# Attention, a 1.58-bit feed-forward and retention joined into one loop over tiles

## The chip, the cores and the metric

The kernel runs on one core of a Trainium2 chip. A core has five engines that work side by side, each through its own instructions in order: TensorE (PE, matrix products and transposes, with weight loads listed apart as PEld), VectorE (DVE), ScalarE (ACT), GpSimd (POOL) and SyncE (SP, which issues transfers). They share the on-chip memory SBUF; products go into PSUM[...]. The metric is the device time of one execution in microseconds (us); lower is better.

## The reference

Four layers, each a gated cross attention and a gated feed-forward, are added onto x, 16 sequences of 128 tokens by 256 features in 32-bit floats. The change touches the second layer and the first half of the third:

```python
x = x + tanh(g_xattn[0]) * L0_xattn(ctx, ctx, layernorm(x), ...)   # long convolution
x = x + tanh(g_ffn[0])   * L0_ffn(layernorm(x), ...)               # mixture of 8 experts, 2 per token
x = x + tanh(g_xattn[1]) * L1_xattn(layernorm(x), ctx, ctx, mask)  # grouped attention, 16 heads on 4
x = x + tanh(g_ffn[1])   * L1_ffn(layernorm(x), w1, w2, w3)        # 1.58-bit feed-forward
x = x + tanh(g_xattn[2]) * L2_xattn(layernorm(x), ctx, ctx, decay) # retention
x = x + tanh(g_ffn[2])   * L2_ffn(layernorm(x), ...)               # mixture of 8 experts, 2 per token
x = x + tanh(g_xattn[3]) * L3_xattn(layernorm(x), ctx, ...)        # attention, 16 heads of 8
x = x + tanh(g_ffn[3])   * L3_ffn(layernorm(x), ...)               # mixture of low-rank experts

# L1_ffn, d = 256, hidden 704
act_quant(x)    = clip(round(x * s), -128, 127) / s,  s = 127 / max(max|x| over a row, 1e-5)
weight_quant(w) = clip(round(w * s), -1, 1) / s,      s = 1 / max(mean|w|, 1e-5)
bitlinear(x, w) = act_quant(x) @ weight_quant(w).T
L1_ffn(x) = bitlinear(silu(bitlinear(x, w1)) * bitlinear(x, w3), w2)

# L2_xattn: a running sum over the 128 tokens of a sequence
r[t] = decay * r[t-1] + ctx[t] * ctx[t]
out[t] = layernorm(x)[t] * r[t]
```

## The kernel before

x stays in SBUF for the whole run as 16 tiles (one a sequence, 128 tokens on the partitions, 256 features). Each half layer is a stage with pools of its own, and the stages follow one another in `passage`: the long convolution (`stage_l0x`), the first mixture (`stage_moe0`), grouped attention (`stage_l1x`), the 1.58-bit feed-forward (`stage_l1f`), retention (`stage_l2x`), the second mixture (`stage_moe2`), the last attention and the last mixture. Most stages write the order of PE, DVE and ACT out by hand (`tc.manual_schedule`): an engine does its instructions in the order in which the functions below are called. POOL's and SP's instructions are placed by the scheduler. A second passage follows only where a flag asks for it.

`stage_l1x` is a loop over steps n. A step does for several tiles a part of the work each: statistics and normalisation of tile n + 4 (`stats`, with the collecting of the first mixture's results, L736, `normal`, L1032), for each pair of tiles the transposes and queries (`turn_x`, `queries`, L1050), the scores and their Exp of tile n (`weigh`, L1092 and L1095, in two halves of two PSUM banks each), the mix with the values of tile n - 1 (`mix`, L1101), its normalisation (`normalise`, L1109 to L1114), the turn and output product of tile n - 2 (`turn_o`, L1120; `output`, L1129 and L1131). Scores use two PSUM buffers of two banks (pool `pss`), everything else four of one bank (pool `pst`). Beside it, one piece a step, `quant_weights` loads the feed-forward's three weight matrices (L1189), sums their absolute values (L1198) and rounds them to -1, 0 and 1 in three DVE instructions each (L1208, L1212, L1220).

`stage_l1f` is a loop of its own with three PSUM buffers of two banks and two of one: statistics on DVE, the reciprocal root on POOL (L1259), normalisation on POOL (L1262), largest absolute value (L1266) and scale, rounding on ACT by adding a large constant (L1281), transposes (L1290) and a copy that takes the constant away (L1294), two products up (L1304), Silu on ACT (L1317), gate on DVE (L1320), largest value and scale (L1322 to L1325), rounding of the hidden rows on ACT (L1330), six transposes (L1337), copy (L1341), product down (L1347) and output (L1351).

`stage_l2x` has no order by hand: it squares the transposed context on ACT (L1388), makes a decay row (POOL L1384, DVE L1386), scans along time on DVE (L1390), and for each pair of tiles transposes the result (L1399), multiplies (L1405) and adds (L1406); its layer norm is the shared helper (L155 to L163). The second mixture's weights (`moe2_weights`, L134 and L141, six transfers from POOL's queue) are held back by `after_all` until the attention's output of tile 5.

## Time and profile before

| What | us |
|---|---|
| median of 3 runs (lowest, highest) | 1083.84 (1081.39, 1085.41) |
| time of the profiled execution | 1083.83 |
| its span | 1082.1 |
| attention: first scores to end of last output | 349.3 to 477.1 |
| feed-forward: its own loop | 477.1 to 566.5 |
| retention | 566.5 to 599.2 |
| second mixture's first DVE instruction | 599.2 |
| all of PE, DVE, ACT, POOL busy, share of the span | 83%, 56%, 40%, 34% |

The profile's page shows each engine's busy share in 40 equal slices, 27 us each. Attention, feed-forward and retention lie in slices 13 to 22:

```profile
PE   3899978999999999966652558899169999998796
DVE  5988867322225465448979859554346555435342
PEclk9999989999999999988995557999569999998899
```

A digit is the busy share in tenths. PE and DVE change places: where PE reads 9, DVE reads 4 to 6, and where DVE reads 7 to 9, PE falls to 6, 5 and 2. The last row is the clock that PE was granted.

### The profile page before, as it was taken

How to read it: one execution, taken by the hardware profiler on the slowest of the kernel's cores; microseconds unless marked ns; L12 is line 12 of the kernel's file. 1: busy time of each engine (PE TensorE's matmuls, PEld its weight loads, DVE VectorE, ACT ScalarE, POOL GpSimd, SP SyncE). 2: the span in 40 equal slices, each digit the busy share in tenths (PEclk: the TensorE clock that was granted, in tenths of full speed). 3: DMA queues.
4: the chain of work that ended last, by engine and by line, in shares of the span. 5: the costliest groups of instructions: out<-in, count | busy, mean ns of one | idle time of the engine just before them, and what ended most of it. 6: DMA issues, size and time to landing. Idle time of an engine off the chain costs nothing. (4 is left out here: it accounts for less than half of the span.)

```text
span 1082.1 us, 14956 instructions
## 1 busy us (share of the span) xinstructions
PE 900.1 (83%) x5212; PEld 595.4 (55%) x5212; DVE 610.3 (56%) x1508; ACT 436.2 (40%) x662; POOL 366.3 (34%) x417
## 2 busy tenths in 40 slices
PE   3899978999999999966652558899169999998796
PEld 1444466777778445424432558788145555555564
DVE  5988867322225465448979859554346555435342
ACT  2111033233322444437760134455257888881111
POOL 5756232643024334035511116650443343201000
PEclk9999989999999999988995557999569999998899
DMA  9100080233223109000000100443489787620000
GB/s 310 34 0 1 0 233 6 78 107 105 65 66 122 40 30 200 1 0 1 1 1 0 59 19 26 151 147 88 124 227 271 216 230 204 169 62 1 20 30 32
DMA packets 71403, 94.13 MB, mean 87 GB/s; under 512 B 9271, under 2 KB 63127, under 8 KB 69015
## 3 DMA queue, kind: packets, MB, share of 16 engines
q1 hardware_dynamic: 56952, 67.21, 20.8%
q0 software_dynamic: 14080, 23.78, 10.3%
q10 hardware_dynamic: 288, 2.10, 0.5%
q8 instruction: 45, 0.74, 0.3%
q14 instruction: 38, 0.31, 0.1%
HBM read 57.06 MB, written 33.55 MB: 84 GB/s over the span
## 5 line engine op out<-in xcount | busy, mean ns | idle before, releaser
L1634 ACT ACTIVATE pt<-s 128x1024 f32<-128x1024 f32 x128 | 127.2, 1024 | 27.5 <-PE s L1627 23.8
L717 POOL DMA_INDIRECT yc<-ys,pos x64 | 62.1, 971 | 129.5 <-DVE x L736 55.2
L297 PE MATMUL y<-kv,toep 128*128 128x512 f32 x192 | 85.7, 597 | 2.3 <-DVE toep L237 2.3
L1643 PE MATMUL av<-pt,v 128*32 128x256 f32 x1024 | 69.4, 389 | 0.1
L289 POOL TENSOR_TENSOR kv<-ctxT 128x1024 f32<-128x1024 f32 x32 | 60.1, 1898 | 27.5 <-PE y L297 27.5
L1627 PE MATMUL s<-qa,ka 64*128 64x256 f32 x512 | 64.9, 334 | 3.4 <-ACT pt L1634 2.7
L1627 PEld LDWEIGHTS s<-qa,ka 64*128 64x128 f32 x512 | 39.0, 190 | 41.5 <-issue 18.3
L297 PEld LDWEIGHTS y<-kv,toep 128*128 128x128 f32 x192 | 35.5, 190 | 44.4 <-issue 41.0
L1654 DVE COPY avs<-av 128x256 f32<-128x256 f32 x64 | 27.1, 423 | 56.4 <-PE av L1643 55.4
L601 POOL DMA_INDIRECT xb<-xs,who x40 | 38.1, 952 | 41.1 <-PE tb L613 32.9
L624 PE MATMUL ub<-L0we,xbT 128*128 x160 | 50.7, 460 | 0.2 <-ACT xbT L615 0.2
L920 PE MATMUL yb<-L2we,hT 88*128 (+1 forms) x224 | 41.2, 312 | 6.4 <-DVE hT L744 4.6
L855 POOL DMA_INDIRECT xb<-xs,who x40 | 38.1, 952 | 24.9 <-PE tb L867 14.9
L1534 POOL TENSOR_TENSOR hl<-f,hl 128x512 fp32r<-128x512 f32 x16 | 20.5, 1280 | 74.3 <-ACT hl L1533 74.3
L302 DVE TENSOR_TENSOR pr<-y,qT 128x1024 f32<-128x1024 f32 x32 | 39.0, 1222 | 11.2 <-PE y L297 9.4
L1095 ACT ACTIVATE pt<-s 128x1024 f32<-128x1024 f32 x32 | 32.8, 1024 | 25.3 <-PE s L1092 25.2
L485 PE MATMUL up<-L0s,xT 128*128 128x352 f32 x128 | 42.5, 477 | 0.0
L920 PEld LDWEIGHTS yb<-L2we,hT 88*128 88x128 f32 x224 | 33.2, 202 | 13.2 <-DVE hT L744 10.1
L305 DVE TENSOR_REDUCE oT<-pr 128x128 f32<-128x1024 f32 x32 | 38.9, 1220 | 1.0
L1643 PEld LDWEIGHTS av<-pt,v 128*32 128x32 f32 x1024 | 26.9, 110 | 20.5 <-issue 0.9
L650 PE MATMUL yb<-L0we,hTb 88*128 x160 | 37.9, 379 | 0.0
L624 PEld LDWEIGHTS ub<-L0we,xbT 128*128 128x128 f32 x160 | 28.8, 190 | 13.2 <-ACT xbT L615 0.5
(383 smaller groups left out, 2031.1 us busy)
## 6 DMA issues: line engine op xcount, KB each, us to landing
scr<-hl SPq DMA_DIRECT2D x64, 256.0 KB, 2.6
ys<-ysb SPq DMA_DIRECT2D x40, 256.0 KB, 2.1
qa<-scr SPq DMA_DIRECT2D x32, 256.0 KB, 4.7
ka<-scr SPq DMA_DIRECT2D x32, 256.0 KB, 5.2
L2we<-in_L_w_dram POOLq DMA_DIRECT2D x6, 792.0 KB, 7.1
L0we<-in_L_w_dram SPq DMA_DIRECT2D x6, 704.0 KB, 7.2
xs<-xn SPq DMA_DIRECT2D x8, 512.0 KB, 4.0
ctxT<-in_ctxT_dram ACTq DMA_DIRECT2D x2, 1024.0 KB, 5.9
```

The costliest lines, as they stand in the source:

```text
L289: nc.gpsimd.tensor_tensor(t, bc(ch, 3, 8), bc(ch, 2, 8), ALU.mult)
L297: nc.tensor.matmul(y[:, ns], lhsT=T[:, h, d : d + P], rhs=kv[mc][:, ns], start=(mc == 0), stop=(mc == lc))
L302: nc.vector.tensor_tensor(pr, y.rearrange("p (b j i) -> p b j i", b=B, j=8), bc(qT[:, lc, :, hs], 2, 8), ALU.mult)
L305: nc.vector.tensor_reduce(oT[:, lc, :, hs], pr, AX.X, ALU.add)
L485: nc.tensor.matmul(t[:, n, 0 : 2 * I], lhsT=xT[:, c, b * P : (b + 1) * P], rhs=s13[:, c, n, :], start=(c == 0), stop=(c == 1),)
L601: nc.gpsimd.indirect_dma_start(out=xbs[s][:, i, :], out_offset=None, in_=xs, in_offset=bass.IndirectOffsetOnAxis(ap=who[:, 2 * s + i : 2 * ...
L624: nc.tensor.matmul(t[:, i, 0 : 2 * I], lhsT=xbT[:, i, c, :], rhs=we[:, bass.ds(regs[s][i] + c * 2 * I, 2 * I)], start=(c == 0), stop=(c == 1),
L717: nc.gpsimd.indirect_dma_start(out=got[b][:, i, :], out_offset=None, in_=ys, in_offset=bass.IndirectOffsetOnAxis(ap=pos[:, i, b : b + 1], ...
L920: nc.tensor.matmul(y[:, i, :], lhsT=hT[:, x, k, i, :], rhs=we[0:HI, bass.ds(at[i] + 4 * I + k * D, D)], start=(n == 0), stop=(n == 3),)
L1627: nc.tensor.matmul(s[:, h, jj, :], lhsT=ka[r, 2 * i + jj, sc * P : (sc + 1) * P], rhs=qa[r, 2 * i + jj, :], start=True, stop=True,)
L1634: nc.scalar.activation(pts[b, i][:, sc], s, AF.Exp)
L1643: nc.tensor.matmul(av[c : c + 32, :], lhsT=va[:, sc, 8 * h + 2 * i + jj, :], rhs=pt[:, sc, h, jj, :], start=(sc == 0), stop=(sc == 1),)
```

## The change

The two loops after the attention go away as stages of their own. `following` gives two functions that the attention's loop calls in each of its steps: `begun(n)`, which quantises the weights in steps 1 to 5, squares the context in steps 1 and 2, makes decay and scan in steps 6 and 7 and issues the second mixture's weights in step 8; and `then(m, place)`, which at four places of a step does the feed-forward and retention of a pair of tiles, by a table `order` of (distance, place). A pair starts every second step and passes through six distances. The loop runs four steps longer. In detail:

- the feed-forward's normalisation goes from POOL to DVE;
- the products up are made in halves of 352 columns (first and third weights side by side in one buffer), so Silu and gate come as four instructions a pair of tiles, twice two halves;
- products up and hidden transposes take the attention's two score buffers; the other products and transposes take its four small ones;
- small scales of two tiles are made in one instruction, and retention multiplies and adds by tile, not by pair;
- three matrices and the decay rows lie in the space of the first mixture's weights, smaller tiles in that of its transposed input; context, its square and the scan share one place;
- the second mixture's weights wait for no chosen instruction, but for the space that the matrices and decay rows held.

```diff
-    def stage_l1x(wq, wo, ka, vbuf, collect, work, pieces):
+    def stage_l1x(wq, wo, ka, vbuf, collect, work, follow):
...
-            for n in range(-4, B + 3 + e):
+            begun, then = follow(pss, pst)
+            for n in range(-4, B + 7 + e):
                 p, odd = divmod(n, 2)
                 fill()
                 when(turn_o, n - e - 2)
+                then(n - e, 0)
...
                 when(stats, n + 4)
                 when(mix, n - e - 1)
+                then(n - e, 1)
...
+                then(n - e, 2)
                 when(output, n - e - 2)
                 when(weigh, n - e, 0)
                 if not odd:
                     when(queries, p + 1, 0, n=B // 2)
                 when(normalise, n - e - 1)
                 when(weigh, n - e, 1)
-                if pieces and not work:
-                    pieces.pop(0)(pst)
...
+                if n >= 0:
+                    begun(n)
+                then(n - e, 3)
...
+            def begun(n):
+                if n == 0:
+                    assert not work
+                    layout()
+                elif n < 4:
+                    total(n - 1)
+                    if n < 3:
+                        squared(n - 1)
+                    else:
+                        size()
+                elif n == 4:
+                    integers(0)
+                    integers(1)
+                elif n == 5:
+                    integers(2)
+                elif n < 8:
+                    decayed(n - 6)
+                    scanned(n - 6)
+                elif n == 8:
+                    l2we.append(moe2_weights())
...
+            def integers(i):
...
+                nc.vector.tensor_scalar(flat[i], flat[i], v["sum"][:, i, 1:2], MAGIC, ALU.mult, ALU.add)
+                nc.vector.tensor_scalar(flat[i], flat[i], MAGIC, 1.0, ALU.subtract, ALU.min)
+                nc.vector.tensor_scalar(w.rearrange("p n w -> p (n w)"), flat[i], -1.0, None, ALU.max)
...
+            def up(q, i):
+                a13 = v[f"a13{q % 2}"]
+                for n in range(2):
+                    t = pss.tile([P, 2, 512], F32, name="fu", tag="s")
+                    for k in range(2):
+                        for c in range(2):
+                            nc.tensor.matmul(
+                                t[:, k, 0:352],
+                                lhsT=v["xT"][:, c, i * P : (i + 1) * P],
+                                rhs=wq[k][:, c, n * 352 : n * 352 + 352],
+                                start=(c == 0),
+                                stop=(c == 1),
+                            )
+                    nc.scalar.activation(v[f"sil{n}"], t[:, 0, 0:352], AF.Silu, scale=a13[:, 0, i : i + 1])
+                    nc.vector.scalar_tensor_tensor(
+                        v[f"hid{i}"][:, n * 352 : n * 352 + 352],
+                        t[:, 1, 0:352],
+                        a13[:, 1, i : i + 1],
+                        v[f"sil{n}"],
+                        ALU.mult,
+                        ALU.mult,
+                    )
...
+            def turn_hidden(q, i):
+                t = pss.tile([P, 8, P], F32, name="fh", tag="s")
+                for n in range(6):
+                    nc.tensor.transpose(t[:, n, :], v[f"hid{i}"][:, n * P : (n + 1) * P], ident)
+                nc.scalar.activation(v[f"hT{i}"], t[:, 0:6, :], AF.Identity, bias=v["magic"][:, 1:2])
...
+            def retain(q):
+                t = pst.tile([P, 2, 2, P], F32, name="fr", tag="a")
+                for i in range(2):
+                    b = 2 * q + i
+                    for c in range(2):
+                        nc.tensor.transpose(t[:, i, c, :], ctxT[:, c, b * P : (b + 1) * P], ident)
+                x = x_of(q)
+                for i, xn in enumerate(rn.pop(q)):
+                    nc.vector.tensor_tensor(xn, xn, t[:, i].rearrange("p c s -> p (c s)"), ALU.mult)
+                    nc.vector.scalar_tensor_tensor(x[:, i, :], xn, tg[:, 2:3], x[:, i, :], ALU.mult, ALU.add)
...
+            order = {
+                (0, 3): [lambda q: stats(q, "f")],
+                (1, 0): [lambda q: normal(q, "f", [v["xn"][:, i, :] for i in range(2)]), largest],
+                (1, 1): [rounded],
+                (1, 3): [turn],
+                (2, 0): [lambda q: up(q, 0)],
+                (2, 1): [lambda q: up(q, 1)],
+                (3, 0): [lambda q: hidden(q, 0), lambda q: hidden(q, 1)],
+                (3, 1): [lambda q: turn_hidden(q, 0)],
+                (3, 2): [lambda q: turn_hidden(q, 1)],
+                (4, 2): [down],
+                (5, 0): [lambda q: stats(q, "r")],
+                (5, 1): [retain_normal],
+                (5, 3): [retain],
+            }
+
+            def then(m, place):
+                for (d, at), fs in order.items():
+                    q, odd = divmod(m - 3 - d, 2)
+                    if at == place and not odd and 0 <= q < B // 2:
+                        for f in fs:
+                            f(q)
```

## The prediction

> **What bounds the kernel now.** I read the page's slices first, then busy time by stretch around the change, then the waits inside those stretches. Columns of the stretches: length, busy time of PE, PE's weight loads, DVE, ACT and POOL (instructions in brackets), granted PE clock, DMA share, GB/s.
>
> ```profile
> 376.00:392.00 16.00, 15.95 (x74) 7.79 (x72) 10.56 (x27) 7.43 (x12) 4.43 (x5) 1.00 0.08 24
> 497.00:547.00 50.00, 35.18 (x243) 24.14 (x241) 46.20 (x138) 36.95 (x50) 25.55 (x48) 0.98 0.00 1
> 477.00:566.50 89.50, 54.34 (x352) 35.66 (x352) 70.73 (x208) 56.04 (x74) 42.50 (x76) 0.91 0.00 1
> 566.50:599.20 32.70, 8.11 (x32) 6.14 (x32) 30.59 (x43) 3.70 (x2) 5.97 (x5) 0.50 0.00 0
> ```
>
> Three limits follow one another. One pair of attention tiles (first row, two steps of the loop) has PE without a gap and DVE at 66%. The feed-forward has DVE at 92% in its steady part and over its 89.5 us PE at 61%. Retention is DVE alone. After the attention's last output (it ends at 477.1) 122 us pass until the second mixture's first DVE instruction at 599.2. The waits, in the attention (first line) and in the feed-forward's steady part (the others), show who is slack; columns: who waited for whom, us in total, times, longest.
>
> ```profile
> DVE xn L1032 <- POOL rs L1023: 16.3, 10, 2.3
> PE y L1347 <- ACT hT L1341: 8.3, 10, 1.1
> PE th L1337 <- ACT hq L1330: 6.1, 10, 1.1
> DVE hid L1320 <- ACT sil L1317: 1.1, 2, 0.7
> ```
>
> In the attention DVE waits 1.6 us each time for POOL's power (POOL issues two gathers first). In the feed-forward PE waits for ACT and DVE, never the reverse for long. A timeline of ACT at the feed-forward's start (start, length, what) gives a price that the new order will pay often:
>
> ```profile
> 487.94 1.09 ACT L1281 ACTIVATE xq<-xn,magic,inv 128x256 f32<-128x256 f32 x2 [1.68 <-DVE inv L1270]
> 489.05 1.28 ACT L1317 ACT_TABLE_LOAD   x1
> 490.34 0.85 ACT L1317 ACTIVATE sil<-ph,a 128x704 f32<-128x704 f32 x1
> ```
>
> Exp and Silu need different tables; before, each stage switches once.
>
> **What the Trainium skill says.** "ScalarE: Activation LUTs", What ACT_TABLE_LOAD costs: a switch is a load of about 1283 ns and a drain of about 1380 ns. The load agrees (1.28 us); the Silu starts 0.01 us after it, so no drain is paid here, and I take 1.28. "TensorE: Matmul & The Clock Gate", Part 1: an idle array drops to half clock and regains it under load. It agrees: 0.50 in retention, 1.00 in the attention. "Perfetto Trace Analysis", Optimization Strategy: a gap that repeats on the engine that should be full can mean too few PSUM buffers. No stretch before shows it, but the change puts the feed-forward into the attention's two score buffers.
>
> **The change, part by part.** The attention's steps 4 to 17 get the other two stages' work, a pair of tiles every two steps; steps 18 to 22 finish it. On PE's first work of a step (its turn of the output, L1120) I read where steps start: 4 at 379.1, 8 at 410.6, 14 at 457.9, 16 at 469.8. A steady attention pair thus takes 15.75 us, the pair of 14 and 15 takes 11.9, the last 7.3.
>
> PE, added per pair of tiles: 4 turns of x, 12 of the hidden and 4 of the retained, at 0.11 us (six take 0.64): 2.2; 16 products up at 0.15 (eight take 1.2): 2.4; 12 down at 0.09 (six take 0.55): 1.1. Together 5.7; a full pair is 15.75 + 5.7 = 21.5.
>
> DVE per pair: the attention's own is 10.56 less two weight sums of 1.61, so 7.3. Added: two statistics at 1.3 (two of 0.42, two of 0.18, one 0.17) 2.6; two normalisations of two tiles at 0.41, 1.65 (the feed-forward's was POOL's, 1.23 each; that relief of POOL is worth nothing by itself); the largest, 0.68 + 3 x 0.17 = 1.2; the gate in halves, 4 x 0.58 (between the same operation's 0.48 at 256 and 0.95 at 704), two maxima at 0.88, three small at 0.16: 4.55; two outputs 0.96; retention 2 x 0.42 + 2 x 0.48 = 1.8. Sum 12.75, with the attention's 20.0. Two of the powers stand right before their use (0.9 and 1.2 us): 22.1. So DVE passes PE and becomes the bound of the mix.
>
> ACT per pair: 7.4 + 6.9 (36.95/50 of 9.3) + 0.3 for halved Silus + two table loads 2.6 = 17.2. Covered by DVE's 22.1, but the load lies between a product up and its gate; the cover is then PE's next product, and uncovered it is 1.28 us a pair.
>
> Steady pair: the feed-forward alone kept DVE 92% busy, so 22.1/0.92 = 24.0, and 0.5 for the table load: 24.5. The single pairs:
> Steps 4, 5: PE 15.75 + 0.4 + 2.4 = 18.6. In step 4 DVE rounds two weight matrices at once, 2 x (1.09 + 1.03 + 0.88) = 6.0, and PE's first product up waits for them, 5.5 after the turn that covers it; the third matrix (2.9) costs 1.5 more. 26.
> Steps 6, 7: DVE 7.3 + 0.8 + 1.2 + 4.55 + 1.0 + 1.3 = 16.1 and two decays and scans, 2 x (1.28 + 4.41) = 11.4: 27.5, taken as 28.
> Steps 8 to 11: 2 x 24.5 = 49.
> Steps 12, 13: no more collecting and normalising for the attention (4 x 0.48, 1.5 and 0.8): DVE 15.8, so PE bounds: 21.5/0.92 = 23.5.
> Steps 14, 15: PE 11.9 + 5.7 = 17.6; with waits 19.5.
> Steps 16, 17: little attention is left; a pair's own chain bounds, from its power to the turned input 7 us, then the products up through two buffers, their maximum and scale 7, and two of waits: 16.
> Sum 162. Start at 379.1 + 2 (two squares of 1.9 us on ACT in steps 1 and 2, between an Exp and the copies that PE needs; at least 0, at most 4): 381. Step 17 ends at 543.
>
> The tail is the last pair alone: 7 to its turned input; 7 for the products up (each half goes 0.6 on PE, 0.48 ACT, 0.58 DVE with three hand-offs, 2.2 us through two buffers, so 1.1 a half) with maximum and scale; 7 for two roundings (0.97), turns, copies (0.90), 12 products and two outputs; 5 for statistics, power, normalisation and retention; 1 for a PE at half clock. 27. The end is 570 against 599.2: 29 us gone. The profiled execution took 1083.83 (span 1082.1), as good as the median 1083.84: 1083.83 - 29 = 1055.
>
> Bounds of the unknown: DVE without any gap. Its work from 379 on is now 52.7 (376 to 477) + 70.7 + 30.6 = 154, and 10 more (16 normalisations 6.6, cut instructions 3.4): 164. Less the tail's 20, 144 after 381, and 27: 552, a gain of 47. That is the best. The worst is priced under the rivals.
>
> Edits at nothing: the weights of the second mixture are issued after step 7's scan, about 435, instead of 410 to 423. They took until 440 (DMA was full from 400 to 440) and the first use is at 629.9, so 130 us cover them. On POOL's queue six issues of 1.04 us and the wait for the scan stand before later gathers; three gather buffers cover a step. If not, 5 us. The weights to be rounded go into the first mixture's space, free since its last product at 309. Padding and decay memsets, 1.9 us of POOL, lie under the start. What follows from 599 on isn't touched and moves as a whole; its first PE work runs at half clock as before, since the tail leaves PE mostly idle.
>
> **Rivals.** First: DVE is packed densely, because the two stages lack each other's stalls. For it: DVE's waits for the attention's products (25.6 us) now have other work in them; against: the clumps in steps 4 to 7 and a strict order. End 554, time 1038. Second: a pair takes 28, since POOL's powers and ACT's tables add to DVE instead of hiding. Five pairs by 3.5 and 5 in the tail: 592, time 1077. Third, slower: the two PSUM buffers that scores, products up and hidden turns share. Each of six hand-offs a pair makes PE wait for ACT and DVE: Silu 0.48, gate 0.58, hand-offs 0.6, about 1.7 us. That is 10 on a mean PE load of 19.8 over seven pairs, 7 x 30 = 210: 381 + 210 + 27 = 618, 19 slower, 1103. It decides from 1.25 us a hand-off (step 17 at 572, so 27.3 a pair and 7.5 of waits). For it: with three such buffers the feed-forward alone already had PE waiting 0.8 us for the hidden copy. Against: attention work stands between most uses, and scores never made PE wait with two. That the stages don't interleave at all is excluded, since the order is written out per step.
>
> **How the numbers follow.** Forecast 1055 (1042 to 1068) 0.56; dense DVE 0.17; 28 a pair 0.15; buffers 0.12. The range leaves out the last and the far half of the dense one: 1034 to 1082. A measurement here tells 0.5%, 5.4 us. Faster: 0.56 + 0.17 + half of 0.15 and a little = 0.82; same 0.05; slower 0.13.
>
> **What would show it.** DVE near 90% and PE near 88% busy from step 8 to 13, with 24 to 25 us a pair; 13 or 14 table loads in the loop; PE idle about 5 us before the first product up; scans followed by a late DVE; the second mixture's first DVE instruction near 570. PE waiting on the gate or the hidden copy over 1 us in most steps would show the third rival; PE at 99% in the mix would show that I overrate DVE's part, and a pair of 28 or more with neither full, that waits in series were underrated.

## The result, and the profile after

The changed kernel takes 1069.1 us (median of 4 runs, 1067.99 to 1071.18), the kernel before on the same chip 1084.05: a ratio of 0.987, with a 95% interval of 0.984 to 0.989. So 15 us are gone where the forecast had 29. In the profiled execution (1067.99 us, span 1066.2) the second mixture's first DVE instruction stands at 583.59 instead of 599.19, which is 15.6 us earlier; the spans differ by 15.9, so what follows it only moved. The loss against the forecast of 570 must therefore lie in the loop and its tail.

The first view of the changed kernel is busy time by stretch, one row for each pair of steps from step 4 on and the last row for the tail. The columns are those of before: stretch, length, PE, PE's weight loads, DVE, ACT, POOL, granted PE clock, DMA share, GB/s.

```profile
383.40:411.20 27.80, 22.86 (x94) 11.05 (x94) 20.54 (x54) 11.54 (x19) 7.21 (x11) 0.73 0.07 19
411.20:439.20 28.00, 22.04 (x116) 12.44 (x117) 23.81 (x52) 17.10 (x25) 7.23 (x11) 0.94 0.07 20
439.20:472.00 32.80, 25.00 (x120) 14.20 (x120) 25.05 (x60) 16.61 (x25) 12.62 (x16) 0.84 1.27 157
472.00:496.20 24.20, 21.36 (x121) 12.55 (x122) 19.05 (x58) 16.57 (x25) 3.86 (x8) 1.00 0.00 1
496.20:519.80 23.60, 21.30 (x121) 12.46 (x121) 15.46 (x46) 16.86 (x25) 2.49 (x6) 1.00 0.00 1
519.80:540.90 21.10, 18.83 (x101) 10.28 (x102) 14.48 (x44) 15.44 (x22) 2.48 (x6) 0.92 0.00 1
540.90:559.20 18.30, 12.64 (x83) 8.48 (x84) 14.47 (x44) 12.33 (x18) 2.48 (x6) 1.00 0.01 2
559.20:583.60 24.40, 12.36 (x72) 8.11 (x69) 18.77 (x53) 9.06 (x13) 3.88 (x8) 0.85 0.00 0
```

The reader sees at once which row stands out. Steps 10 and 11 (fourth row) are the steady pair and take 24.2 us. Steps 8 and 9 (third row) do the same work on the tiles, with the second decay and scan (5.7 us of DVE) besides, and take 32.8. PE is busy 88% of the steady pair and DVE 79%, so no engine is full. Where the clock is under 1.00, the same matmuls also cost PE more time: 25.00 us in the third row, 21.36 in the fourth.

The waits of the same stretches (who waited for whom, us in total, times, longest) name what PE lacked:

```profile
PE s L1083 <- ACT follow L1375: 10.2, 5, 5.8
PE fu L1339 <- DVE follow L1347: 8.3, 7, 2.0
PE fu L1339 <- DVE w1q L1253: 2.4, 1, 2.4
PE fu L1339 <- DVE w3q L1253: 1.9, 1, 1.9
```

Attention scores (L1083) wait for the copy of a hidden turn (L1375), which frees their PSUM buffer; one of five such waits is 5.8 us long. In the kernel before no score waited for a buffer. The timeline around it, in step 8 (start, length, engine and instruction, in brackets the idle time before it and its releaser), shows where the 5.8 us come from:

```profile
438.97 1.28 DVE L1260 TENSOR_SCALAR raws<-raws,dcol 128x2048 f32<-128x2048 f32 x1
440.28 4.42 DVE L1263 TENSOR_TENSOR_SCAN ctxT<-raws,ctxT 128x2048 f32<-128x2048 f32 x1
...
444.63 0.40 DVE L1294 BATCH_NORM_STATS2 follow<-x 128x6 f32<-128x256 f32 x1
445.00 1.13 POOL L134 DMA_DIRECT2D L2we<-in_L_w_dram  x1 [8.60 <-DVE ctxT L1263]
...
446.19 0.73 POOL L1297 TENSOR_TENSOR follow<-follow,neghalf 128x2 f32<-128x2 f32 x1
446.96 1.07 DVE L1303 TENSOR_SCALAR follow<-x,follow 128x256 f32<-128x256 f32 x2 [0.86 <-POOL follow L1297]
448.06 0.69 DVE L1309 TENSOR_REDUCE follow<-follow 128x2 f32<-128x512 f32 x1
...
449.39 1.09 ACT L1320 ACTIVATE follow<-follow 128x256 f32<-128x256 f32 x2 [6.26 <-DVE follow L1312]
450.39 0.88 ACT L1375 ACTIVATE follow<-fh,follow 128x768 bf16<-128x768 f32 x1
451.18 0.57 ACT L1032 COPY xT<-tx 128x512 f32<-128x512 f32 x1
451.32 2.08 PE L1083 MATMUL s<-qa,ka 18*128 18x512 f32 x4 [5.78 <-ACT follow L1375]
453.33 3.64 PE L1041 MATMUL tq<-xT,l1q 128*128 128x256 f32 x8
```

The second decay and scan are written at the end of step 7 and hold DVE until 444.6. Behind them stand the statistics of the next pair, POOL's power, the normalisation and the largest value. ACT's next instruction, the rounding (L1320), needs that largest value, and ACT idles 6.26 us for it. The hidden copy (L1375) has had its data since 443.6, when PE's first hidden turn ended, but stands behind the rounding in ACT's order. So it runs at 450.4, and PE waits until 451.3 for the buffer. The queries (L1041), which come next, take 3.64 us instead of 2.0, at a granted clock of 0.53. That agrees with the Trainium skill, "TensorE: Matmul & The Clock Gate", Part 1: after an idle window the array restarts at half rate. The last two lines of the waits list are the rounding of the weights, for which the first products up wait 4.3 us in step 5. The gate (L1347) makes PE wait about 1.2 us in each odd step.

### The profile page after: what moved, and what is told of

Read it like the earlier page. It is cut to its first block, busy times and chain, and to the rows that moved or that the text cites. A ratio compares the mean times of both kernels' runs of the same rounds, so it can differ in the third digit from the quotient of the medians.

```text
span 1066.2 us, 14873 instructions
## 1 busy us (share of the span) xinstructions
PE 901.7 (85%) x5212; PEld 599.4 (56%) x5212; DVE 613.6 (58%) x1528; ACT 451.9 (42%) x690; POOL 341.0 (32%) x387
## 5 line engine op out<-in xcount | busy, mean ns | idle before, releaser
L1661 ACT ACTIVATE pt<-s 128x1024 f32<-128x1024 f32 x128 | 127.3, 1022 | 27.4 <-PE s L1654 23.5
L707 POOL DMA_INDIRECT yc<-ys,pos x64 | 62.1, 970 | 96.6 <-DVE x L726 56.2
L1681 DVE COPY avs<-av 128x256 f32<-128x256 f32 x64 | 27.1, 423 | 56.7 <-PE av L1670 56.6
L1083 PE MATMUL s<-qa,ka 18*128 18x512 f32 x128 | 37.1, 656 | 10.2 <-ACT follow L1375 10.2
L1561 POOL TENSOR_TENSOR hl<-f,hl 128x512 fp32r<-128x512 f32 x16 | 20.5, 1279 | 74.3 <-ACT hl L1560 74.3
L910 PEld LDWEIGHTS yb<-L2we,hT 88*128 88x128 f32 x224 | 33.6, 205 | 13.5 <-DVE hT L734 10.2
L1670 PEld LDWEIGHTS av<-pt,v 128*32 128x32 f32 x1024 | 27.0, 110 | 20.7 <-issue 1.3
L1086 ACT ACTIVATE pt<-s 128x1024 f32<-128x1024 f32 x32 | 32.3, 1023 | 10.9 <-PE s L1083 10.7
```

Source lines behind the costliest of these rows:

```text
L707: nc.gpsimd.indirect_dma_start(out=got[b][:, i, :], out_offset=None, in_=ys, in_offset=bass.IndirectOffsetOnAxis(ap=pos[:, i, b : b + 1], ...
L910: nc.tensor.matmul(y[:, i, :], lhsT=hT[:, x, k, i, :], rhs=we[0:HI, bass.ds(at[i] + 4 * I + k * D, D)], start=(n == 0), stop=(n == 3),)
L1661: nc.scalar.activation(pts[b, i][:, sc], s, AF.Exp)
L1670: nc.tensor.matmul(av[c : c + 32, :], lhsT=va[:, sc, 8 * h + 2 * i + jj, :], rhs=pt[:, sc, h, jj, :], start=(sc == 0), stop=(sc == 1),)
```

## The experiments

Four theories were held against each other. **A**: a block of DVE work in a single step delays the chain statistics, power, largest, rounding, and PE feels it only through ACT's program order. **B**: POOL's six issues of the second mixture's weights, which fall into step 8, delay the powers. **C**: the table loads between Exp and Silu lie on the path. **D**: the two score buffers, shared with the hidden turns and products up, are too few by themselves.

The runs went in five sets. In sets 2 and 5 the chip's kernel before took 1097.8 and 1098.4 us instead of 1083 to 1085, so only ratios are compared between sets. This table has, for all runs, the length of each pair of steps in the profiled execution, from PE's turn of the output to that two steps later, and the ratio to the kernel before. A star marks a kernel that leaves out or changes part of the computation. Each row shows one execution. Four rows have the loop of the changed kernel ("changed", "changed, again", "issues called later", "issues held"): their pairs differ by up to 1.2 us in steps 4 to 9 and by 1.0 in steps 14 and 15, and by nothing in steps 10 to 13. A smaller difference in one pair says little.

| kernel | 4, 5 | 6, 7 | 8, 9 | 10, 11 | 12, 13 | 14, 15 | ratio (95% interval) |
|---|---|---|---|---|---|---|---|
| changed | 27.8 | 28.0 | 32.8 | 24.1 | 23.6 | 21.1 | 0.987 (0.984 to 0.989) |
| no scan* | 27.6 | 27.5 | 24.6 | 24.1 | 23.6 | 20.1 | 0.978 (0.976 to 0.980) |
| issues called later | 27.6 | 28.0 | 32.5 | 24.1 | 23.6 | 21.1 | 0.987 (0.984 to 0.989) |
| hidden copy first | 27.6 | 29.0 | 30.6 | 23.4 | 22.9 | 18.9 | 0.979 (0.976 to 0.981) |
| scan spread | 28.6 | 27.1 | 25.2 | 24.4 | 23.9 | 21.4 | 0.983 (0.981 to 0.986) |
| Exp for Silu* | 27.8 | 30.9 | 31.9 | 22.9 | 24.2 | 21.7 | 0.986 (0.982 to 0.990) |
| half products* | 27.3 | 29.3 | 33.4 | 23.8 | 22.3 | 20.8 | 0.985 (0.982 to 0.989) |
| short maxima* | 27.6 | 30.2 | 32.8 | 23.2 | 23.1 | 20.6 | 0.980 (0.977 to 0.983) |
| spread all | 27.8 | 28.4 | 24.9 | 24.4 | 23.7 | 18.9 | 0.977 (0.972 to 0.981) |
| changed, again | 28.6 | 29.2 | 33.5 | 24.1 | 23.6 | 20.1 | 0.985 (0.982 to 0.987) |
| rounding late | 27.9 | 27.8 | 29.7 | 23.4 | 22.9 | 18.9 | 0.978 (0.976 to 0.980) |
| even steps | 24.3 | 26.1 | 27.3 | 24.3 | 23.6 | 20.1 | 0.974 (0.972 to 0.976) |
| both | 24.0 | 24.6 | 27.3 | 23.4 | 22.9 | 18.9 | 0.974 (0.972 to 0.976) |
| both, issues held | 24.1 | 25.0 | 24.6 | 23.4 | 22.9 | 18.9 | 0.973 (0.970 to 0.975) |
| issues held | 27.6 | 29.2 | 33.2 | 24.1 | 23.6 | 20.1 | 0.984 (0.981 to 0.986) |
| both, call later | 24.0 | 25.2 | 26.1 | 24.5 | 23.7 | 18.9 | 0.973 (0.970 to 0.976) |
| then Exp* | 23.4 | 23.9 | 25.7 | 21.8 | 22.3 | 17.8 | 0.964 (0.962 to 0.966) |
| then short maxima* | 23.9 | 22.9 | 26.4 | 22.6 | 22.6 | 18.9 | 0.962 (0.960 to 0.964) |
| then half products* | 23.6 | 26.4 | 25.3 | 23.7 | 22.2 | 18.4 | 0.965 (0.963 to 0.968) |

**No scan.** The edit:

```diff
                 elif n < 8:
-                    decayed(n - 6)
-                    scanned(n - 6)
+                    pass
```

> Leaves out the two decays and the two scans of steps 6 and 7 (retention then weighs with the bare squares), 11.4 us of DVE. Theory A (the scans are an unhidden block on DVE, and the second one makes step 8 late through statistics, power, largest, rounding and, behind it in ACT's order, the copy that frees the score buffer): steps 6 and 7 fall from 28 to 22 to 24 us and steps 8 and 9 from 32.8 to 24 to 25, so 12 to 14 us less than the changed kernel, about 1056; PE's clock stays at 1.00 in step 8. Theory B (POOL's six weight issues in step 8 delay the powers): steps 6 and 7 fall by 4 to 5, steps 8 and 9 stay at 30 or more, about 1063. Theory D (the shared score buffers alone): PE's waits before the scores stay at about 10 us, at most 4 us gained, 1065.

1059.98 us. Two rows of its busy time, steps 8 and 9:

```profile
437.03:448.69 11.66, 11.62 (x59) 6.50 (x59) 8.38 (x31) 8.96 (x14) 5.00 (x8) 0.85 0.14 35
448.69:461.67 12.98, 10.73 (x63) 6.19 (x63) 10.48 (x28) 7.56 (x12) 0.84 (x2) 1.00 0.00 0
```

Step 8 falls from 20.1 to 11.66 with PE full, and the pair by 8.2 us. That is the whole gain in time within its error (9 us). The surprise is steps 6 and 7, where the scans are written: 0.5 us, not the 4 to 6 that A expected. The first scan and decay, 5.7 us written at the end of step 6, nearly have room beside PE. They fill step 7, where DVE was busy 13.74 of 14.12 us and which takes 13.14 without them. The second, which stands in front of the next pair's statistics, is the dear one. Since the scan's end also released the buffer of the weights, POOL's issues moved to steps 6 and 7 here. So this run alone does not exclude B, and the issues may hide a little of what steps 6 and 7 gained; in "scan spread" below, with short scans and the issues after the loop, the pair takes 27.1.

**Issues called later.** The call of moe2_weights was moved from step 8 to step 12.

```diff
-                elif n == 8:
+                elif n == 12:
                     l2we.append(moe2_weights())
```

> The loads of the second mixture's weights are issued in step 12 instead of step 8; nothing else moves. Theory A: steps 8 and 9 stay within 2 us of 32.8 and the whole within 3 of 1069. Theory B: steps 8 and 9 fall to about 25, the whole to about 1061, and steps 12 and 13 may take part of it back. The weights still have over 80 us before their first use, so no wait of the second mixture is expected by either.

1068.59 us, and the pair 32.5. It agrees with A, but the trace shows that the issues hardly moved, so it tested nothing. The first issue stands at 443.7 us, where it was at 445.0:

```profile
L134 POOL DMA_DIRECT2D L2we<-in_L_w_dram x4: 1045/1052/1132, 443.7 to 454.4; - x4
```

PE, DVE and ACT run in the written order in this stage, while POOL's order is planned: an issue goes where its buffer is free, wherever the text has it. The run named "issues held" repeats this test.

**Issues held.** To hold the buffer, one DVE instruction on two columns of it was added in step 12:

```diff
-                elif n == 8:
+                elif n == 12:
+                    nc.vector.tensor_scalar(raws[:, 0:2], raws[:, 0:2], 1.0, None, ALU.mult)
                     l2we.append(moe2_weights())
```

> The changed kernel, with the buffer of the second mixture's weights kept in use until step 12 by one tiny DVE instruction, so that POOL's six issues cannot come before about 507 us. Theory A: step 8 stays at 19 to 20 us (the power waits for DVE behind the scan, issues or not), the whole within 3 us of the changed kernel, 0.982 to 0.987 of the kernel before. Theory B: step 8 falls to 13 or less, 0.977.

Now the issues stand from 507.9 us on. Steps 8 and 13 of this kernel:

```profile
439.73:460.23 20.50, 13.85 (x58) 8.19 (x59) 14.14 (x32) 8.96 (x13) 5.00 (x8) 0.75 0.05 14
508.48:520.69 12.21, 10.70 (x65) 6.16 (x63) 8.93 (x22) 7.70 (x12) 5.93 (x7) 1.00 2.12 291
```

Without an issue in it (DMA share 0.05 instead of 1.30) step 8 still takes 20.5 us. Step 13, which now has the six issues and the transfer at 291 GB/s, takes 12.21 as it does without them. B is excluded as the cause of the miss, and the ratio 0.984 agrees with the changed kernel's.

**Hidden copy first.** On ACT alone the order of two instructions is exchanged:

```diff
-                (1, 1): [rounded],
...
                 (3, 1): [lambda q: turn_hidden(q, 0)],
+                (1, 1): [rounded],
```

> On ACT the copy of the first hidden turn is put ahead of the rounding of the next pair's input, in every second step; the computation is the same. Theory A with D (the copy that frees a score buffer stands behind a rounding that waits for DVE): PE's waits before the scores fall from 10.2 us to under 4; steps 8 and 9 lose 3 to 5 of 32.8, the steady pairs 0.7 to 1 each; 5 to 9 us in all, about 1062. If the scans alone set step 8 (DVE has to do the work anyway and PE only waits somewhere else), the wait moves to the turned input of the feed-forward or to the queries and the gain is under 2 us, 1067 to 1069.

1061.85 us, 7 us less than the changed kernel, within what A with D expected. But steps 8 and 9 lose only 2.2 of the 8.3 by which they exceed the forecast: step 8 still takes 17.94. With the buffer freed in time, the scores run, and the next thing in line comes late, the copy of the attention's turned input (L1032), which in ACT's order also stands behind the rounding. PE waits 5.7 us for it. The rest of the gain comes in small parts: 0.7 in each steady pair, 1.2 to 2.2 in steps 14 and 15 (the changed kernel's two profiles differ there). The scores wait for the hidden copy no more at all.

**Rounding late.** So the rounding was put behind all three copies:

```diff
-                (1, 1): [rounded],
...
                 (3, 2): [lambda q: turn_hidden(q, 1)],
+                (1, 2): [rounded],
```

> One edit: ACT's rounding of the next pair's input goes behind both hidden copies and behind the attention's copy of its turned input, instead of ahead of all three. Theory A in its present form (a late DVE reaches PE only through ACT's program order; a block of DVE work at the end of an odd step delays the statistics, the power, the largest and so the rounding): steps 6, 8 and all later even steps fall, 8 from 20.1 to 14 or 15, the steady even steps from 11.4 to 10.6, PE keeps its full clock in step 8; 9 to 12 us less than the changed kernel, 0.977 of the kernel before, more than with the first hidden copy alone. If the turned input then comes too late for the products up, odd steps grow by about 1 us and the gain is 5.

1058.72 us against 1067.81 for the changed kernel on the same chip: 9.1 us gained, at the lower end. Step 8 and the even step of the steady pair:

```profile
438.67:454.80 16.13, 12.80 (x59) 7.01 (x59) 14.58 (x33) 8.99 (x14) 7.86 (x11) 0.84 1.12 158
468.36:479.04 10.68, 10.54 (x59) 6.30 (x59) 8.36 (x30) 9.06 (x14) 3.01 (x6) 1.00 0.06 11
```

The steady even step is now PE from end to end: 10.54 of 10.68. Step 8 misses its expectation of 14 to 15 by over a microsecond and runs at a clock of 0.84, not 1.00. The attention's own DVE work still queues behind the scan: PE waits 3.0 us for DVE's sum of the attention's output into x (L1122). ACT's order carries much of the delay to PE, not all of it.

**Scan spread.** One scan for each pair of tiles, on 256 columns, with the decay row made once for one pair:

```diff
+            def scanned(q):
+                for c in range(2):
+                    u = ctxT[:, c, q * 2 * P : q * 2 * P + 2 * P]
+                    nc.vector.tensor_tensor_scan(
+                        u, dk[1][:, c * 2 * P : c * 2 * P + 2 * P], u, 0.0, ALU.mult, ALU.add
+                    )
...
+                (4, 3): [scanned],
```

> The scan is cut into one piece per pair of tiles and half, issued after the pair's products down, and the decay row is made for one pair only and used for all: DVE does 16 scans of 256 columns (estimated 4.42/8, about 0.6 us each with its start-up) and two short decays, some 10 us in place of 11.4, of which 1.2 in each pair. Theory A: steps 6 and 7 fall to 23 to 24, steps 8 and 9 to 24.5 to 25.5, later pairs grow by at most 0.5 each; 8 to 12 us less than the changed kernel, 1057 to 1061. Theory B: steps 8 and 9 stay over 30, about 1064. If DVE's sum bounds a pair, the gain of the early steps comes back in the later ones, 1.2 a pair, and the whole gains 3 to 5.

1065.94 us: steps 8 and 9 recover as A said (25.2), and the 1.27 us of scans per pair cost later pairs 0.3. But the whole gained only 3 us. That is the number of the third case in the expectation, met for another reason: the tail grew by 8. The first instruction of the second mixture stands 42.4 us after the start of step 17, in the changed kernel 34.6. POOL's timeline of this kernel near the end shows why:

```profile
569.98 0.71 POOL L1302 TENSOR_TENSOR follow<-follow,neghalf 128x2 f32<-128x2 f32 x1 [3.32 <-DVE follow L1301]
575.43 4.14 POOL L134 DMA_DIRECT2D L2we<-in_L_w_dram  x4 [4.74 <-DVE ctxT L1267]
579.57 2.12 POOL L140 DMA_DIRECT2D L2we<-in_L_w_dram  x2
581.70 0.73 POOL L1302 TENSOR_TENSOR follow<-follow,neghalf 128x2 f32<-128x2 f32 x1
```

The decay row lies in the buffer that the second mixture's weights take over. With the last scan at the end, the six issues wait for it and then stand for 6.3 us ahead of the last pair's power, for which DVE waits 5.9 us. So B's mechanism exists, but here, not in step 8.

**Exp for Silu, half products, short maxima.** Three runs on the changed kernel took work from ACT, PE and DVE in turn, to see what limits the steady pair.

```diff
-                    nc.scalar.activation(v[f"sil{n}"], t[:, 0, 0:352], AF.Silu, scale=a13[:, 0, i : i + 1])
+                    nc.scalar.activation(v[f"sil{n}"], t[:, 0, 0:352], AF.Exp, scale=a13[:, 0, i : i + 1])
```

> ACT computes Exp where the feed-forward asks for Silu, so the gate is another function, and no table is loaded inside the loop (14 or more loads of 1.28 us fall away). Theory C (the loads lie on the path): a pair falls by 1.3 to 2.6, over seven pairs and the tail 10 to 18 us, 1051 to 1059. My prediction's price (0.5 a pair): 4 us, 1065. If other work covers the loads entirely: within 1 us of 1069. Steps 8 and 9 stay over 30 in every case.

```diff
-                        for c in range(2):
+                        for c in range(1):
...
-                    for n in range(6):
+                    for n in range(3):
```

> The feed-forward's products add up half of what they should: one of two channel groups going up, three of six hidden groups going down, which takes 8 products of 0.15 and 6 of 0.09 from PE, 1.75 us a pair. If PE with its weight loads bounds the steady pair (88% busy): steps 10 to 13 fall by 1.7 to 2 a pair, the whole by 12 to 14, about 1056. If DVE bounds it, as the prediction had it: under 0.5 a pair, 1066 or more. If waits in series bound it, what lies on the chain from turned input to gate counts, about half: 0.8 a pair, 1063.

```diff
-                nc.vector.tensor_reduce(am, v["xn"], AX.X, ALU.max, apply_absolute_value=True)
+                nc.vector.tensor_reduce(am, v["xn"][:, :, 0:32], AX.X, ALU.max, apply_absolute_value=True)
...
-                    hm[:, 0, i : i + 1], v[f"hid{i}"][:, 0:HID], AX.X, ALU.max, apply_absolute_value=True
+                    hm[:, 0, i : i + 1], v[f"hid{i}"][:, 0:32], AX.X, ALU.max, apply_absolute_value=True
```

> The three maxima of a pair (over the normalised input and over each hidden tile) look at 32 values a row only, so the scales are others; DVE has 2 x 0.8 + 0.5 = 2.1 us less to do in a pair. If DVE bounds the steady pair: steps 10 to 13 fall by 2.1 to 2.3 a pair, the whole by 15, 1054. If PE bounds it: under 0.5 a pair, 3 in all, 1066. If the chain does, part of it: the maximum over the input stands between the power and ACT's rounding, the others before the hidden rounding, 1 a pair and 2 in the tail, 1060.

Ratios 0.986, 0.985 and 0.980; the first two can't be told from the changed kernel's. None reached the 10 us or more that its own bound would give. The odd steps 9 and 11 fall by 1.2 us each without table loads, but step 12 is then 1.7 us longer, at a clock of 0.87 instead of 1.00, which hides it. Step 6 is 1.6 to 2.8 us longer in all three runs; why stays open. These three were inconclusive as to sizes and are repeated below on a kernel without the long gaps.

**Spread all.** Hidden copy first, scan spread with the decay row in a buffer of its own, and the weight sums, scale and rounding one piece a step:

```diff
+                    total(0)
+                elif n < 3:
+                    total(n)
...
+                elif n < 6:
+                    integers(n - 3)
```

> Three edits together: the hidden copy ahead of the rounding; one scan of 256 columns per channel group in each pair, its decay row in a buffer of its own, so that the second mixture's weights do not wait for the last scan; and weight sums, scale and rounding one piece a step from step 0 to 5, so that no step has more than 3.1 us of them. Theory A (blocks of DVE work in single steps cause the misses of steps 4 to 9, the ACT order carries them): steps 4 and 5 fall from 27.8 to 22 to 23, 6 and 7 from 28 to 24, 8 and 9 to 24, later pairs as with the copy first plus 0.3; 16 to 20 us less than the changed kernel, about 1051. If the blocks were already paid for by the first one alone, the sum is smaller than the parts: the copy first and no scan alone gave 7 and 9, and about 1058 would come out.

1071.16 us where the kernel before took 1097.83. The ratio 0.977 isn't told from that of the hidden copy alone. Steps 8 and 9 recover (24.9), but steps 4 to 7 don't fall at all: 27.8 and 28.4. That the pieces are small did not help. The timeline of step 4 of this kernel shows where they stand:

```profile
383.92 0.94 DVE L1251 TENSOR_SCALAR raws<-raws,follow 128x1408 f32<-128x1408 f32 x1
384.89 0.89 DVE L1252 TENSOR_SCALAR raws<-raws 128x1408 f32<-128x1408 f32 x1
385.82 0.89 DVE L1253 TENSOR_SCALAR w1q<-raws 128x1408 bf16<-128x1408 f32 x1
386.63 0.42 DVE L1297 BATCH_NORM_STATS2 follow<-x 128x6 f32<-128x256 f32 x1
...
390.98 1.09 ACT L1323 ACTIVATE follow<-follow 128x256 f32<-128x256 f32 x2 [3.98 <-DVE follow L1315]
391.98 0.56 ACT L1032 COPY xT<-tx 128x512 f32<-128x512 f32 x1
...
392.59 3.78 PE L1041 MATMUL tq<-xT,l1q 128*128 128x256 f32 x8 [3.77 <-ACT xT L1032]
```

It is step 8 again on a smaller scale. A rounding of 2.7 us at the end of an odd step is ahead of the statistics, ACT's rounding is late by it, and the copy behind it makes PE idle 3.77 us and then run at a clock of 0.50. So theory A needs a correction: the place of a block counts more than its size. What ends an odd step delays this chain; what ends an even step should not, and the next run puts that to the test.

**Even steps.** With ACT's order left as in the change, all blocks were moved to even steps; decay row and scans as in the run before, with the scans at the end of even steps:

```diff
-                elif n < 4:
-                    total(n - 1)
...
+                    for i in range(3):
+                        total(i)
+                elif n == 1:
+                    size()
...
+                elif n == 2:
+                    integers(0)
...
                 elif n == 4:
-                    integers(0)
                     integers(1)
-                elif n == 5:
+                elif n == 6:
                     integers(2)
-                elif n < 8:
-                    decayed(n - 6)
-                    scanned(n - 6)
+                    for c in range(2):
+                        decayed(c)
...
+                (3, 3): [scanned],
```

> No block of DVE work stands at the end of an odd step any more: weight sums in step 0, scale in 1, the three roundings in steps 2, 4 and 6, short decays in 6, one pair's scans in each even step; ACT's order stays that of the changed kernel. Theory A: steps 4 to 9 lose their misses, 27.8 + 28 + 32.8 become 22 + 24 + 24.5, 18 us less, 0.971 of the kernel before. If the amount of DVE work matters and not its place, steps 4 to 7 stay at 27 each and only steps 8 and 9 gain, as without the scan: 9 us, 0.979.

1053.58 us, 14.2 less than the changed kernel on the same chip (forecast 18). Its pairs of steps 4 to 11:

```profile
381.44:405.75 24.31, 19.08 (x93) 10.63 (x93) 17.40 (x48) 11.56 (x19) 7.20 (x11) 0.93 0.07 22
405.75:431.82 26.07, 22.37 (x116) 12.95 (x117) 20.40 (x54) 17.69 (x27) 10.42 (x14) 0.93 0.82 122
431.82:459.07 27.25, 23.80 (x121) 13.23 (x121) 20.27 (x60) 16.06 (x24) 9.22 (x13) 0.87 0.71 93
459.07:483.35 24.28, 22.27 (x120) 12.73 (x121) 20.16 (x60) 16.64 (x25) 3.86 (x8) 0.93 0.00 1
```

The same sums, scale and roundings, three pieces of about 2.8 us in steps 2, 4 and 6 instead of 3, 4 and 5, make steps 4 to 7 5.8 us shorter than in "spread all" (the scans moved from odd to even steps as well, and the hidden copy stands late again). In steps 4 to 7 PE waits 6.2 us for the copy L1032 there and 1.8 here, and little for the rounded weights in both (0.3 and 0.5). This is the clearest evidence for the corrected theory.

**Both,** the even steps with the late rounding:

> The two edits together. With no late DVE left the order of ACT is worth only its steady part, 0.7 us a pair: 18 + 4 = 22 us less than the changed kernel, about 0.967 of the kernel before. If the two were independent it would be 28, 0.961; if both only moved the same wait, 18, 0.971.

1053.84 us: in time no more than the even steps alone, under the 4 us expected on top, though its profiled loop (steps 2 to 16) is 165.0 us against 169.6. The gain over the changed kernel is 14 us, where the two alone had 9.1 and 14.2, so in time they remove largely the same wait. Steps 8 and 9 were left at 27.3. The weights' issues had moved to steps 7 and 8 with their buffer's release. In step 8 DVE waits 3.5 us once for the attention's power, which stands on POOL behind three gathers (L707). The issues may have pushed these back. A run with the call moved to step 12 does not test it, as its issues stayed at 424 us:

> The version with both edits, and the loads of the second mixture's weights issued in step 12 instead of step 8. If POOL's six issues hold up the attention's power there (3.5 us of waiting in step 8): steps 8 and 9 fall from 27.2 to 24, the whole by 3 us, 0.971 of the kernel before. If they only move the wait to step 12: no change, 0.974. If the weights then come too late: slower.

0.973 (0.970 to 0.976). Then the buffer was held as above:

> The version with both edits, and the buffer kept until step 12. If the issues hold up the attention's power in step 8: steps 8 and 9 fall from 27.2 to 24 and steps 12 and 13, where no attention power is left, do not grow; 3 us, 0.971 of the kernel before. If the wait only moves to step 12 and 13: no change, 0.974. If the weights come too late for the second mixture: slower.

```profile
437.50:449.14 11.64, 11.56 (x58) 6.43 (x59) 8.51 (x31) 8.87 (x14) 5.00 (x8) 0.86 0.08 24
449.14:462.13 12.99, 10.73 (x63) 6.19 (x63) 11.42 (x30) 7.58 (x12) 0.85 (x2) 1.00 0.00 0
496.19:508.40 12.21, 10.70 (x64) 6.17 (x63) 9.13 (x23) 7.70 (x12) 5.94 (x7) 1.00 2.11 289
```

Steps 8 and 9 fall to 24.6, DVE's wait for that power to 1.8, and step 13, which takes over the issues, does not grow. No step of 8 to 13 is now much off its steady length. The ratio 0.973 (0.970 to 0.975) is, with that of the later call, the lowest of the kernels that compute the same. It beats the kernel before and the changed one, but "both" and even steps alone, 0.974, can't be told from it by time.

**What limits a steady pair.** The three removals again, each on the run with both edits and the later call (1055.06 us in this set):

> On the version with all edits, ACT computes Exp where Silu is asked for, so the gate is another function, and the loop has no table loads. If a load stands on the path of each odd step (between the product up and its gate): odd steps 9, 11 and 13 fall by 1.2 us each from 12.7 and 12.2, even steps stay at 10.7; about 8 us in all. At my prediction's price of 0.5 a pair: 3.5. If covered: none.

> On the version with all edits, the three maxima of a pair look at 32 values a row only, so the scales are others; DVE has 2.1 us less in a pair. If DVE bounds the steady pair: 2 us a pair, 14 in all. If waits do: 0.5 a pair, in the odd steps, where a maximum of the first hidden tile stands ahead of the next gate; 4 with the tail.

> On the version with all edits, the products up add one of two channel groups and those down three of six hidden groups; PE has 1.75 us less in a pair, all of it in odd steps. If PE bounds: odd steps fall by 1.7 and the whole by 12. If the odd steps are a chain through the table load and the gates: 0.3 in steps 9 and 11, as on the changed kernel, and 2 to 3 in all.

They took 1044.33, 1042.32 and 1045.59 us, 10.7, 12.7 and 9.5 us less. By the whole time alone each of the three engines could pass for a bound. By step it is told apart; these are step 11 of the reference, of Exp, of the short maxima and of the half products, one fence each:

```profile
472.11:484.81 12.70, 10.70 (x64) 6.15 (x63) 10.66 (x29) 7.28 (x12) 0.84 (x2) 1.00 0.00 1
```

```profile
464.91:476.42 11.51, 10.66 (x64) 6.10 (x63) 11.09 (x30) 5.62 (x11) 0.84 (x2) 1.00 0.00 1
```

```profile
466.65:478.86 12.21, 10.71 (x64) 6.16 (x63) 9.19 (x29) 7.70 (x12) 0.84 (x2) 1.00 0.00 1
```

```profile
468.64:481.05 12.41, 9.02 (x50) 4.79 (x49) 10.67 (x29) 7.23 (x12) 0.84 (x2) 0.99 0.01 2
```

One load less on the path gives 1.2 us, 1.5 us less of DVE 0.5, and 1.7 us less of PE 0.3. In step 13, where the attention collects no more, the reference's 12.20 become 11.13, 12.21 and 10.85: there PE's products count as well. The load's place shows in PE's second set of products up in step 11, in the reference and without the loads:

```profile
476.34 0.46 PE L1345 MATMUL fu<-w1q,follow 128*128 128x352 bf16 x2 [1.03 <-DVE follow L1353]
```

```profile
468.05 0.47 PE L1345 MATMUL fu<-w1q,follow 128*128 128x352 bf16 x2
```

The wait of 1.03 us for the gate is gone; from the queries (L1041) to the end of the step only 0.1 us changes. So the odd step is a series of waits, from the product up over load, Silu and gate to the next product and, at its end, for DVE, and no engine bounds it. The even step of "both" is PE's: 10.54 of 10.68 us. Much of the three gains is not explained by this: in the profiled executions 1.9 to 4.4 us of them lie in steps 2 to 8 and 2.4 to 4.2 after the start of step 17. Part is the clock: the profiled reference ran steps 6, 10 and 12 at 0.85 or 0.86 (11.81 us in step 10), the short maxima at 1.00 (10.40). What decides the clock there stays open.

## Why the prediction was wrong

It said 29 us and 15 came. The direction and the place were right, but 1069.1 lies just outside the 1042 to 1068 of the main forecast, though inside the wide range of 1034 to 1082. One term of the sum carries most of the miss, and one reason was wrong although its numbers fit. In the order of its steps (predicted, measured, us):

| step of the sum | predicted | measured |
|---|---|---|
| start of step 4 | 381 | 383.4 |
| steps 4, 5 | 26 | 27.8 |
| steps 6, 7 | 28 | 28.0 |
| steps 8, 9 | 24.5 | 32.8 |
| steps 10, 11 | 24.5 | 24.1 |
| steps 12, 13 | 23.5 | 23.6 |
| steps 14, 15 | 19.5 | 21.1 |
| steps 16, 17 | 16 | 18.3 |
| tail | 27 | 24.4 |
| second mixture begins | 570 | 583.6 |

**The failed step** is "Steps 8 to 11: 2 x 24.5 = 49", together with "two decays and scans, 2 x (1.28 + 4.41) = 11.4: 27.5" in the line above it. The durations were right (1.28 and 4.42 in the trace). But they were booked as an amount of DVE work in the pair in which they are written, and the next pair was taken as steady. In fact a scan inside steps 6 and 7 cost little (28.0 with, 27.5 without), and the one that ended step 7 cost 8.2 us in steps 8 and 9. That pair alone is 8.3 of the 13.6 us by which the end was missed. "Scans followed by a late DVE" stood among the signs to look for; whose work queues behind the scan, on DVE and then on ACT, wasn't followed.

**Steps 6 and 7 at 28** were right by accident. What makes them long is, as far as the runs tell, the third rounding at the end of step 5. Step 6 takes 13.89 with it and 14.35 without the scans; where it was moved the pair takes 26.1, and 24.6 and 25.0 with the late rounding on ACT besides. These runs moved the scans too, so the share of each stays open. Steps 4 and 5 were priced by the right mechanism. PE waits there 2.4 and 1.9 us for the rounded weights, where 5.5 were booked for the first two matrices; but PE also ran at a clock of 0.73 over the pair, which was not, and the sum came out 1.8 over.

**DVE as the bound** was wrong. It was busy 79% in the steady pair (19.05 us where the sum had 20.0; with two waits for a power of 0.83 us each it is 20.7, where the sum had 22.1). The odd half of the pair of 24.1 comes from waits in series, as the three removals showed, and its even half from PE with waits of 0.8 us. The factor 1/0.92 had been taken from a stretch with another limit; that it met the right size was luck.

**Table loads**: 13 in the loop, as forecast, 1.28 us each. Priced at 0.5 a pair; the measured price is 1.2. Of that 1.1 is the one load between product up and gate, while the other, ahead of the Exp at the step's end, cost 0.1 (step 11). In all seven loads ahead of a Silu, the load did not start before the data of its Silu were there (here 0.67 us of idle for the product, then the load, then the Silu):

```profile
485.17 1.28 ACT L1346 ACT_TABLE_LOAD   x1 [0.67 <-PE fu L1339]
486.47 1.00 ACT L1346 ACTIVATE follow<-fu,follow 128x352 f32<-128x352 f32 x2
```

The Trainium skill, "ScalarE: Activation LUTs", What ACT_TABLE_LOAD costs, has the load's length right here (about 1283 ns); the drain that it adds isn't seen, as the Silu starts 0.02 us after the load. The load's place on the path is what the run without it adds.

**The rest**: step 4 started 4.3 us later than before (383.4 instead of 379.1), where 2 were booked for the squares, with a bound of 4. PE's wait for the weight sums ahead of their scale, 1.7 us, wasn't in the sum. Steps 14 to 17 were 3.9 longer than taken, and the late rounding alone gets 1.2 to 2.2 of them back (18.9 in steps 14 and 15), so ACT's order was part of it. The tail was 2.6 shorter than its hand-offs priced.

**The rivals.** Dense DVE didn't come: DVE reached 85% in steps 6 and 7 and at most 79% in every other pair. The pair of 28 was reached in steps 4 to 9 but for another reason, and the steady pair did not show it. The shared buffers are half true: PE waited 10.2 us on the hidden copy, but more than half of that in one step with a late DVE, and these waits are gone when only ACT's order is changed, with the same two buffers (in step 8 most of the wait then moved to another copy). More buffers weren't tried.

## What to carry to other kernels

In this kernel a block of work on an engine with slack was free or dear by its place more than by its size. Ask which short chain queues behind it, and which instructions of the next engine stand in program order behind that chain's end, for it was their release that PE waited for. When stages are merged, price the step after the block, and put blocks where the next link of the chain is furthest away. A queue whose order is planned apart from the text is moved by its buffers, so read from the trace that an experiment moved what it meant to move.

## What was not expected of the hardware

The same step at PE busy from end to end ran at two clocks: step 10 took 10.68 us at 1.00 in the profile of "both" and 11.81 at 0.86 in that of the run with the later call, with PE busy 10.54 and 11.76 us. The text of the two differs only in a POOL call for a later stage. So a fall of the clock cost 1 us in a step with no long gap in it; what brought it on isn't shown. After the long gap in step 8 the cost was larger: 3.64 us for eight products that take 2.0 otherwise.

And an issue on POOL kept what follows it waiting while it waited for its buffer: 8.6 us in the changed kernel (the bracket at 445.00 above), harmless there, as step 8 was as long with the issues elsewhere, and 4.74 us ahead of the last power in "scan spread", where DVE had to wait for it.
